# Two attention averages of one group, taken one step apart and gathered bank by bank

## The chip, the cores and the metric

The kernel runs on one core of a Trainium2 chip. Times are device microseconds of one execution, as a median of several runs; less is better. The trace comes from one further execution under the hardware profiler.

## The reference

The model is a two-layer perceiver block on 16 batches of 64 latents (width 128). Each layer has a cross-attention of the latents onto a context of 1601 rows (16 heads), then a sequence layer (a selective scan) and a feed-forward part (a mixture of experts in layer 0, quantised in layer 1). The part that the change touches is the cross-attention:

```python
xn = layernorm(context); ln = layernorm(latents)
q = ln @ Wq
k, v = split(concat([xn, ln]) @ Wkv)
w = softmax(q k^T * scale)          # per batch and head; 64 latents x 1665 keys
out = (w @ v) @ Wo
```

## The kernel before, in words

**Tiling.** Keys and queries are folded, so that scores are taken between the normalised context (transposed, `kvT`, width 128) and 8 heads x 64 latents = 512 query columns at a time. A "group" is one layer, one batch and one half of the heads: 2 x 16 x 2 = 64 groups. A group has NT = 13 key tiles of 128 rows (the last one holds 64 context rows and the 64 latents; the 1601st context row is treated apart, through `ee` and `xeb`).

**One step.** `run` (L1419) walks over steps n; step n handles tile i = n mod 13 of group g = n div 13 and calls `step` (L1562). It first issues the scores of that tile (`scores`, L643): one matmul of 512 columns into one of three PSUM banks tagged "s"; VectorE folds it into a running maximum R (L664 with a mask in layer 1, L666 without); ScalarE copies it into half of a two-tile buffer tagged "st2" (L669 or L671). There are eleven st2 buffers (and two for the single thirteenth tile). When the group is through, its maximum is transposed and reduced (`maximum`, L674, at step 1 of the next group), spread (L698, step 3), and subtracted from the stored scores, which are then exponentiated in place (`weigh`, L701: VectorE L706, ScalarE L707), a pair of tiles at a time on every second step.

**The averages.** LAG = 21 steps behind the scores, `average` (L709) multiplies the exponentials of a tile with the context rows: four matmuls of 128 queries x 129 columns (width 128 and a column of ones for the denominator), accumulated over the group's 13 tiles. Two of the four blocks lie in one PSUM bank and two in another, and both banks are one tile, `av`, of which there is one. After the thirteenth tile, `gather` (L721) adds the row treated apart and moves the four blocks to SBUF (four VectorE instructions, L728). The first tile of a group is not averaged in its own step but together with the second (`ia` 0 and 1). Seen by the step's position in the 13, the last averages of a group are in step 7, step 8 has none, and step 9 has those of tiles 0 and 1 of the next group.

**After it.** Thirteen steps behind, `denominator` (L764: reciprocal on VectorE, product on Pool), `turn` (L770: four transposes) and, after each second batch, `output` (L785: 32 matmuls, L791, and VectorE's sum into X, L795) follow at fixed steps. The last group of all has its own end, `finish` (L732).

**What sets the order.** `scores` and `average` are issued in the text's order; the compiler's planner then orders each engine's instructions by its own model, as far as data and the hand-made ordering edges (`behind`, L1545) allow. Background work is put between: preparation of contexts by due step (`prep`), and the sequence and feed-forward layers, once their inputs are done (`between`, with due steps from `done`, L1426). A batch's context lies in `kv`, of which there are three buffers; the next load (`context_load`, L468, with Pool's memset L472 and SP's DMA L486 or L489) waits until the averages of three batches before are through. In layer 0, `context` (L576) then begins with VectorE's reduce over the rows loaded (L606).

Of the kernel before, what the change touches and what calls it, by code (L numbers as in the profile page):

```python
# [32 lines left out]
F32 = mybir.dt.float32  # L33
# [4 lines left out]
ALU = mybir.AluOpType  # L38
# [4 lines left out]
P = 128  # L43
NB, L, D = 16, 64, 128
# [8 lines left out]
NT = G + 1  # L53
NQ = 512
LAG = 21
# [24 lines left out]
class Kernel:  # L80
# [236 lines left out]
    def raw_pair(self, lay, l, r, g, queue):  # L317


        if lay == 0:  # L320
            t = self.at.tile([P, 2, NQ], F32, tag="st2", name=f"raw{l}{g}", bufs=11)
            pair = [t[:, i, :2 * D].rearrange("p (m d) -> p m d", m=2) for i in range(2)]
        else:
            pair = [self.at.tile([P, 2, D], F32, tag="raw", name=f"raw{n}{g}", bufs=3) for n in (l, r)]
        for t, n in zip(pair, (l, r)):
            queue.dma_start(out=t, in_=self.a[f"L{lay}{n}"].rearrange("(m p) d -> p m d", p=P)[:, 2 * g:2 * g + 2, :])
        return pair
# [140 lines left out]
    def context_load(self, lay, b):  # L468
        nc = self.nc
        kv = self.at.tile([P, G + 1, D + 1], F32, tag="kv", name=f"kv{lay}_{b}", bufs=3)  # L470
        kvT = self.at.tile([P, SK + L], F32, tag="kvT", name=f"kvT{lay}_{b}", bufs=2)
        nc.gpsimd.memset(kv[:, :, D:], 1.0)  # L472
        if lay == 0:
            ctxd = self.a["ctx"]
            tiles = ctxd[b, :P * G, :].rearrange("(p g) d -> p g d", g=G)
            nc.gpsimd.memset(kv[64:P, G, :D], 0.0)
            if b == 0:

                self.raw_kv = [self.at.tile([P, 2, NQ], F32, tag="st2", name=f"rkv{j}", bufs=11).rearrange("p i (g d) -> p (i g) d", d=D) for j in range(2)]
                for lo in range(0, G, 4):  # L480
                    nc.sync.dma_start(out=self.raw_kv[lo // 8][:, lo % 8:lo % 8 + 4, :], in_=tiles[:, lo:lo + 4, :])
                    if lo == 0:
                        self.raw0.append(self.raw_pair(0, "WqT", "WkT", 1, nc.sync))
                nc.sync.dma_start(out=self.raw_kv[1][:REM, G - 8, :], in_=ctxd[b, P * G:SK, :])
            else:
                nc.sync.dma_start(out=kv[:, :G, :D], in_=tiles)  # L486
                nc.sync.dma_start(out=kv[:REM, G, :D], in_=ctxd[b, P * G:SK, :])
        else:
            nc.sync.dma_start(out=kv[:, :, :D], in_=self.xh[b])  # L489
            nc.sync.dma_start(out=kvT[:, :SK], in_=self.xhT[b])  # L490
        self.kv_of[lay, b] = (kv, kvT)

    def first_context(self):


        nc = self.nc
        kv, kvT = self.kv_of[0, 0]
        w1 = self.vecs_of(0)[0]
        n = G + 1
# [22 lines left out]
        def turned(lo, hi):  # L522
            m, w = (P, (hi - lo) * P) if hi < n else (REM, REM)
            t = self.tp(f"kt0_{lo}")
            for k in range(lo, hi):
                nc.tensor.transpose(t[:, (k - lo) * P:(k - lo) * P + m], kv[:m, k, :D], self.ident[:m, :m])

            for i, j in ((0, P), (P, w)) if lo == 0 else ((0, w),):
                nc.scalar.activation(kvT[:, lo * P + i:lo * P + j], t[:, i:j], AF.Copy, scale=self.vcol[:, w1:w1 + 1])
            raw = self.at.tile([P, 2, NQ], F32, tag="st2", name=f"xt{lo}", bufs=11)[:, 0, :w]  # L530
            nc.vector.tensor_copy(raw, t[:, :w])
            nc.sync.dma_start(out=self.xhT[0][:, lo * P:lo * P + w], in_=raw)

# [109 lines left out]
    def scores(self, g, i):  # L643

        nc, grp = self.nc, self.groups[g]
        lay, b, half = grp["key"]
        if i == 0:
            grp["st"] = []
            grp["R"] = self.at.tile([P, NQ], F32, tag="R", name=f"R{g}", bufs=2)
        if i % 2 == 0:  # L650
            n = min(2, NT - i)
            grp["st"].append(self.at.tile([P, n, NQ], F32, tag=f"st{n}", name=f"st{g}_{i // 2}", bufs=11 if n == 2 else 2))
        st, R = grp["st"][i // 2][:, i % 2, :], grp["R"]
        q = self.q_of[lay, b][:, half * 8:half * 8 + 8, :].rearrange("p h l -> p (h l)")
        s = self.pss.tile([P, NQ], F32, tag="s", name=f"s{g}_{i}")
        mm = nc.tensor.matmul(s, self.kv_of[lay, b][1][:, i * P:(i + 1) * P], q, start=True, stop=True)  # L656
        self.place["PE"].append(mm.ins)
        masked = lay == 1
        mc = self.mcol[:, i, b:b + 1] if masked else None

        if i:
            last = grp["st"][0][:, 0, :] if i == 1 else R
            if masked:
                mx = nc.vector.scalar_tensor_tensor(R, s, mc, last, ALU.add, ALU.max)  # L664
            else:
                mx = nc.vector.tensor_tensor(R, s, last, ALU.max)  # L666
            self.place["DVE"].append(mx.ins)
        if masked:
            ev = nc.scalar.activation(st, s, AF.Identity, bias=mc)  # L669
        else:  # L670
            ev = nc.scalar.copy(st, s)  # L671
        self.place["ACT"].append(ev.ins)
# [33 lines left out]
        nc.vector.tensor_tensor(st, st, self.row(mb, [P, n, NQ]), ALU.subtract)  # L706
        nc.scalar.activation(st, st, AF.Exp)  # L707

    def average(self, g, i):  # L709


        nc, grp = self.nc, self.groups[g]
        lay, b, half = grp["key"]
        if i == 0:
            grp["av"] = self.psa.tile([P, 2, NQ], F32, tag="av", name=f"av{g}")
        for k in range(4):
            o = grp["av"][:, k // 2, k % 2 * (D + 1):(k % 2 + 1) * (D + 1)]
            st = grp["st"][i // 2][:, i % 2, k * P:(k + 1) * P]
            nc.tensor.matmul(o, st, self.kv_of[lay, b][0][:, i, :], start=(i == 0 and k % 2 == 0), stop=(i == NT - 1 and k % 2 == 1))  # L719

    def gather(self, g):  # L721

        nc, grp = self.nc, self.groups[g]
        aq = grp["aq"] = self.at.tile([P, 4, D + 1], F32, tag="aq", name=f"aq{g}", bufs=2)
        xeb = self.xeb_of[grp["key"][:2]]
        for k in range(4):
            o = grp["av"][:, k // 2, k % 2 * (D + 1):(k % 2 + 1) * (D + 1)]
            nc.vector.scalar_tensor_tensor(aq[:, k, :], xeb, grp["ee"][:, k:k + 1], o, ALU.mult, ALU.add)  # L728
        for k in ("st", "R", "av", "mb"):
            grp.pop(k)  # L730

    def finish(self, g):  # L732


        nc, grp = self.nc, self.groups[g]
        lay, b, half = grp["key"]
        b1 = self.vecs_of(lay)[1]
        aq = self.at.tile([P, 4, D + 1], F32, tag="aq", name=f"aq{g}", bufs=2)
        xeb, av = self.xeb_of[lay, b], grp["av"]
        blocks = av[:, :, :2 * (D + 1)].rearrange("p k (j d) -> p k j d", j=2)  # L740
        four = lambda v: v.rearrange("p (k j) -> p k j", k=2)
        den, rd = self.sm([P, 4], "den"), self.sm([P, 4], "rd")
        nc.vector.tensor_tensor(four(den), blocks[:, :, :, D], four(grp["ee"]), ALU.add)
        nc.vector.reciprocal(rd, den)
        turned = []
        for k in range(4):
            nc.vector.scalar_tensor_tensor(aq[:, k, :D], xeb[:, :D], grp["ee"][:, k:k + 1], blocks[:, k // 2, k % 2, :D], ALU.mult, ALU.add)
        for k in range(4):
            nc.scalar.activation(aq[:, k, :D], aq[:, k, :D], AF.Copy, scale=rd[:, k:k + 1])
            at = self.pss.tile([P, NQ], F32, tag="s", name=f"at{g}_{k}") if k < 3 else self.tp(f"at{g}_{k}")  # L750
# [7 lines left out]
            else:  # L758
                nc.scalar.activation(to, at, AF.Identity, bias=self.vcol[:, b1:b1 + 1])
        self.output(lay, b // 2, 1)  # L760
        for k in ("st", "R", "av", "mb"):
            grp.pop(k)

    def denominator(self, g):  # L764
# [654 lines left out]
    def run(self, out):  # L1419
# [3 lines left out]
        ng = len(self.groups)  # L1423
        per_layer = NB * 2 * NT
        start = lambda lay, b: lay * per_layer + b * 2 * NT
        done = lambda lay, b: start(lay, b) + LAG + 9  # L1426
        self.place = {"PE": [], "ACT": [], "DVE": [], "SP": [], "Pool": []}
        ahead = self.setup()

# [35 lines left out]
                    if next(between[0][2], None) is None:  # L1465
                        between.pop(0)

        self.summed, self.upto_sums = False, upto_sums
        n, go, budget, finished = 0, 0, 0.0, 0
        while n < (ng + 1) * NT + LAG + 8 or between:  # L1470
            for lay in range(2):
# [90 lines left out]
    def step(self, n, ng):  # L1562
# [1 line left out]
        if g < ng:  # L1564
            self.scores(g, i)

        ga, ia = divmod(n - LAG, NT)
        if 0 <= ga < ng and ia:
            if ia == 1:
                self.average(ga, 0)  # L1570
            self.average(ga, ia)
            if ia == NT - 1:
                if ga == ng - 1:
                    self.upto_sums()
                    self.finish(ga)
                else:
                    self.gather(ga)

        for p in (g - 2, g - 1):
            o = n - (p + 1) * NT  # L1580
# [12 lines left out]
        if 0 <= d < ng:  # L1593
            lay, b, half = self.groups[d]["key"]
            if d == ng - 1:
                return
            with self.behind():
                if o == 0:
                    self.denominator(d)
                elif o == 4:  # L1600
                    self.turn(d)
                if o == 7 and b % 2 and half:
                    self.output(lay, b // 2)
                elif o == 9 and d == ng - 2:
                    self.output(lay, b // 2, 0)


# [55 lines left out]
```

## Time and profile before

| what | value |
|---|---|
| median of 3 runs | 1988.09 us (1985.63 to 1988.84) |
| the profiled execution's own time | 1984.66 us |
| its span, first to last instruction | 1983.0 us |
| mean granted TensorE clock | 0.999 |
| averages, L719, 6656 matmuls | 866.3 us busy |
| scores, L656, 1664 matmuls | 850.6 us busy |
| gathers, L728, 252 instructions | 72.0 us busy, 341 ns each |
| subtract, L706 / exponential, L707 | 505.2 us / 445.6 us busy |

How to read it: PE is TensorE's matmul row and PEld its weight loads, which lie beside matmuls; DVE is VectorE, ACT ScalarE, POOL Pool, SP the engine that issues most DMAs. A matmul on 32-bit floats shows as two instructions. In a line such as "s L656 <- ACT st L671" the engine's instruction of line 656, writing tile s, waited for ScalarE's instruction of line 671. Matmuls overlap in their pipeline, so their cost is read from the distance between starts, not from their length.

### The profile page before, as it was taken

To read this page: it belongs to the slowest core of one execution; us is meant where nothing else is said; L and a number is where in the kernel's file an instruction comes from. 1 tells how busy PE (TensorE), PEld (TensorE's weight loads), DVE (VectorE), ACT (ScalarE), POOL (GpSimd) and SP (SyncE) were. 2 spreads that over 40 slices of the span, in tenths; PEclk is the share of its full clock that TensorE was granted. 3 is DMA by queue.
4 is the path that set the end of the run, shared out by engine and by line. 5 is a ranking of instruction groups with operands and counts; after the bars stand their busy time and mean duration, and the time that the engine had idled before them with its cause. 6 is when DMAs were issued, how large, how long until landed. Compare 5 with 4: busy or idle time off the path is not lost. (4 is left out here: it accounts for less than half of the span.)

```text
span 1983.0 us, 32835 instructions
## 1 busy us (share of the span) xinstructions
PE 1938.7 (98%) x12083; PEld 1476.6 (74%) x12083; DVE 1557.6 (79%) x2976; ACT 1380.2 (70%) x2642; POOL 516.1 (26%) x579
## 2 busy tenths in 40 slices
PE   8999999999999999999999999999999999999998
PEld 5777777677777767768777777777778777787787
DVE  6977667977868787775998778898786878777885
ACT  5787778887768888656766667776665656765561
POOL 5211122543113552121542202442110121101000
PEclk9999999999999999999999999999999999999999
DMA  6121112322122121221221112221120211101000
GB/s 178 51 68 43 46 53 77 92 58 70 29 81 85 60 82 53 66 79 45 68 82 53 41 32 71 70 58 53 49 67 2 58 37 37 42 17 37 24 1 22
DMA packets 144110, 110.82 MB, mean 56 GB/s; under 512 B 13762, under 2 KB 130254, under 8 KB 143950
## 3 DMA queue, kind: packets, MB, share of 16 engines
q1 hardware_dynamic: 143406, 108.46, 18.8%
q8 instruction: 96, 1.57, 0.3%
q14 instruction: 64, 0.52, 0.1%
q10 hardware_dynamic: 544, 0.26, 0.0%
HBM read 80.23 MB, written 27.41 MB: 54 GB/s over the span
## 5 line engine op out<-in xcount | busy, mean ns | idle before, releaser
L719 PEld LDWEIGHTS av<-kv,st 128*128 128x128 f32 x6656 | 853.3, 192 | 324.0 <-issue 305.9
L719 PE MATMUL av<-kv,st 128*128 128x129 f32 x6656 | 866.3, 275 | 3.2 <-DVE aq L728 2.5
L656 PE MATMUL s<-qT,kvT 128*128 128x512 f32 x1664 | 850.6, 599 | 16.0 <-ACT st L671 8.7
L707 ACT ACTIVATE st<-st 128x1024 f32<-128x1024 f32 (+1 forms) x448 | 445.6, 999 | 113.2 <-DVE st L706 110.4
L706 DVE TENSOR_TENSOR st<-st,mb 128x1024 f32<-128x1024 f32 (+1 forms) x448 | 505.2, 1133 | 19.8 <-PE mb L698 19.8
L669 ACT ACTIVATE st<-s,mcol 128x512 f32<-128x512 f32 x416 | 283.8, 683 | 217.3 <-DVE R L664 173.5
L671 ACT COPY st<-s 128x512 f32<-128x512 f32 x416 | 240.5, 580 | 132.5 <-DVE R L666 101.1
L656 PEld LDWEIGHTS s<-qT,kvT 128*128 128x128 f32 x1664 | 258.7, 191 | 77.9 <-ACT st L671 28.3
L664 DVE SCALAR_TENSOR_TENSOR R<-s,mcol,R 128x512 f32<-128x512 f32 x352 | 261.8, 744 | 42.3 <-PE s L656 40.8
L666 DVE TENSOR_TENSOR R<-s,R 128x512 f32<-128x512 f32 x352 | 240.5, 683 | 44.4 <-PE s L656 43.7
L570 POOL TENSOR_TENSOR kv<-kv,vec 128x384 f32<-128x384 f32 (+1 forms) x128 | 132.2, 1054 | 169.3 <-DMA xh<-kv 63.9
L768 POOL TENSOR_TENSOR aq<-aq,rd 128x512 f32<-128x512 f32 x63 | 71.4, 1134 | 354.6 <-DVE rd L767 349.3
L872 POOL TENSOR_TENSOR db<-sc_u,bb 128x512 f32<-128x512 f32 x64 | 84.6, 1324 | 141.0 <-DVE h L883 86.1
L889 POOL TENSOR_TENSOR sc_y<-sc_y,h 128x512 f32<-128x512 f32 x60 | 86.0, 1434 | 98.1 <-DVE h L888 81.5
L883 DVE TENSOR_TENSOR_SCAN h<-da,db 128x512 f32<-128x512 f32 x64 | 82.3, 1286 | 0.0
L621 ACT ACTIVATE kv<-kv,coff,crstd 128x128 f32<-128x128 f32 x182 | 76.3, 492 | 4.1 <-POOL coff L618 4.1
L612 ACT ACTIVATE scr<-kv,cmean 128x128 f32<-128x128 f32 x182 | 73.0, 401 | 3.0
L666 DVE TENSOR_TENSOR R<-s,st 128x512 f32<-128x512 f32 x32 | 22.0, 687 | 66.7 <-PE s L656 54.6
L135 POOL TENSOR_TENSOR crstd<-cvar,neghalf 128x13 f32<-128x13 f32 x14 | 34.2, 2440 | 152.0 <-DVE cvar L616 152.0
L728 DVE SCALAR_TENSOR_TENSOR aq<-xeb,ee,av 128x129 f32<-128x129 f32 x252 | 72.0, 341 | 1.0 <-PE av L719 0.8
L455 PE MATMUL q<-xnT,wqk 128*128 128x128 f32 x512 | 69.5, 278 | 0.3
L455 PEld LDWEIGHTS q<-xnT,wqk 128*128 128x128 f32 x512 | 63.1, 192 | 8.5 <-issue 3.0
(409 smaller groups left out, 1927.8 us busy)
## 6 DMA issues: line engine op xcount, KB each, us to landing
bb<-bcd SPq DMA_DIRECT2D x64, 256.0 KB, 4.6
xh<-kv SPq DMA_DIRECT2D x16, 832.0 KB, 4.8
kv<-xh SPq DMA_DIRECT2D x16, 832.0 KB, 5.6
kvT<-xhT SPq DMA_DIRECT2D x16, 800.0 KB, 4.6
xhT<-kvT SPq DMA_DIRECT2D x15, 800.0 KB, 3.4
kv<-in_ctx_dram SPq DMA_DIRECT2D x15, 768.0 KB, 5.5
ew<-in_e1T_dram SPq DMA_DIRECT2D x36, 64.0 KB, 1.8
ew<-in_e3T_dram SPq DMA_DIRECT2D x36, 64.0 KB, 1.9
```

The lines of the kernel that those rows point to most:

```text
L455: nc.tensor.matmul(t[:, k * P:(k + 1) * P], self.wqk[:, g * 4 + k, :], xnT, start=True, stop=True)
L570: nc.gpsimd.tensor_tensor(kv[:, lo:hi, :D], kv[:, lo:hi, :D], self.row(self.vec[:, w1, :], [P, hi - lo, D]), ALU.mult)
L656: mm = nc.tensor.matmul(s, self.kv_of[lay, b][1][:, i * P:(i + 1) * P], q, start=True, stop=True)
L664: mx = nc.vector.scalar_tensor_tensor(R, s, mc, last, ALU.add, ALU.max)
L666: mx = nc.vector.tensor_tensor(R, s, last, ALU.max)
L669: ev = nc.scalar.activation(st, s, AF.Identity, bias=mc)
L671: ev = nc.scalar.copy(st, s)
L706: nc.vector.tensor_tensor(st, st, self.row(mb, [P, n, NQ]), ALU.subtract)
L707: nc.scalar.activation(st, st, AF.Exp)
L719: nc.tensor.matmul(o, st, self.kv_of[lay, b][0][:, i, :], start=(i == 0 and k % 2 == 0), stop=(i == NT - 1 and k % 2 == 1))
L872: nc.gpsimd.tensor_tensor(db, u, self.row(bb[:, 0, s % 2, :], both), ALU.mult)
L889: nc.gpsimd.tensor_tensor(y, y, h, ALU.add)
```

## The change

The tile `av` becomes two tiles of one bank each, `av0` and `av1`. `average` takes the bank j and issues two of the four matmuls. `step` calls it for bank 0 at LAG steps behind the scores and for bank 1 at LAG + 1. `gather` takes the bank too: each bank is gathered (two instructions) right after its own last tile, bank 1 a step after bank 0. For the last group of all, bank 1's last tile is averaged in the same step as bank 0's, and `finish` follows there. `finish` reads the two tiles and computes its denominators in two instructions. There are twelve st2 buffers. `denominator`, `turn`, `output` and the due steps of the background work (`done`) move by one step.

```diff
-            t = self.at.tile([P, 2, NQ], F32, tag="st2", name=f"raw{l}{g}", bufs=11)
+            t = self.at.tile([P, 2, NQ], F32, tag="st2", name=f"raw{l}{g}", bufs=12)
...
-    def average(self, g, i):
+    def average(self, g, i, j):
...
         if i == 0:
-            grp["av"] = self.psa.tile([P, 2, NQ], F32, tag="av", name=f"av{g}")
-        for k in range(4):
-            o = grp["av"][:, k // 2, k % 2 * (D + 1):(k % 2 + 1) * (D + 1)]
-            st = grp["st"][i // 2][:, i % 2, k * P:(k + 1) * P]
-            nc.tensor.matmul(o, st, self.kv_of[lay, b][0][:, i, :], start=(i == 0 and k % 2 == 0), stop=(i == NT - 1 and k % 2 == 1))
-
-    def gather(self, g):
+            t = self.psa.tile([P, NQ], F32, tag=f"av{j}", name=f"av{g}_{j}")
+            grp["av", j] = t[:, :2 * (D + 1)].rearrange("p (k d) -> p k d", k=2)
+        for k in range(2):
+            st = grp["st"][i // 2][:, i % 2, (2 * j + k) * P:(2 * j + k + 1) * P]
+            nc.tensor.matmul(grp["av", j][:, k, :], st, self.kv_of[lay, b][0][:, i, :], start=(i == 0 and k == 0), stop=(i == NT - 1 and k == 1))
+
+    def gather(self, g, j):
...
-        aq = grp["aq"] = self.at.tile([P, 4, D + 1], F32, tag="aq", name=f"aq{g}", bufs=2)
-        xeb = self.xeb_of[grp["key"][:2]]
-        for k in range(4):
-            o = grp["av"][:, k // 2, k % 2 * (D + 1):(k % 2 + 1) * (D + 1)]
-            nc.vector.scalar_tensor_tensor(aq[:, k, :], xeb, grp["ee"][:, k:k + 1], o, ALU.mult, ALU.add)
+        if j == 0:
+            grp["aq"] = self.at.tile([P, 4, D + 1], F32, tag="aq", name=f"aq{g}", bufs=2)
+        xeb, av = self.xeb_of[grp["key"][:2]], grp.pop(("av", j))
+        for k in range(2):
+            nc.vector.scalar_tensor_tensor(grp["aq"][:, 2 * j + k, :], xeb, grp["ee"][:, 2 * j + k:2 * j + k + 1], av[:, k, :], ALU.mult, ALU.add)
...
-        nc.vector.tensor_tensor(four(den), blocks[:, :, :, D], four(grp["ee"]), ALU.add)
+        for j in range(2):
+            nc.vector.tensor_tensor(den[:, 2 * j:2 * j + 2], av[j][:, :, D], grp["ee"][:, 2 * j:2 * j + 2], ALU.add)
...
-        done = lambda lay, b: start(lay, b) + LAG + 9
+        done = lambda lay, b: start(lay, b) + LAG + 10
...
-        ga, ia = divmod(n - LAG, NT)
-        if 0 <= ga < ng and ia:
+        for j in range(2):
+            ga, ia = divmod(n - LAG - j, NT)
+            if not 0 <= ga < ng or not ia:
+                continue
+            end = ga == ng - 1 and ia == NT - 1
+            if j and end:
+                continue
             if ia == 1:
-                self.average(ga, 0)
-            self.average(ga, ia)
-            if ia == NT - 1:
-                if ga == ng - 1:
-                    self.upto_sums()
-                    self.finish(ga)
-                else:
-                    self.gather(ga)
+                self.average(ga, 0, j)
+            self.average(ga, ia, j)
+            if end:
+                self.late_half = ga
+            elif ia == NT - 1:
+                self.gather(ga, j)
+        if self.late_half is not None:
+            self.average(self.late_half, NT - 1, 1)
+            self.upto_sums()
+            self.finish(self.late_half)
+            self.late_half = None
...
-                if o == 0:
+                if o == 1:
                     self.denominator(d)
-                elif o == 4:
+                elif o == 5:
                     self.turn(d)
-                if o == 7 and b % 2 and half:
+                if o == 8 and b % 2 and half:
                     self.output(lay, b // 2)
-                elif o == 9 and d == ng - 2:
+                elif o == 10 and d == ng - 2:
                     self.output(lay, b // 2, 0)
```

More of the change, by code (lines that the diff above doesn't have):

```diff
@@ L477, in context_load @@
             if b == 0:
-                self.raw_kv = [self.at.tile([P, 2, NQ], F32, tag="st2", name=f"rkv{j}", bufs=11).rearrange("p i (g d) -> p (i g) d", d=D) for j in range(2)]
+                self.raw_kv = [self.at.tile([P, 2, NQ], F32, tag="st2", name=f"rkv{j}", bufs=12).rearrange("p i (g d) -> p (i g) d", d=D) for j in range(2)]
                 for lo in range(0, G, 4):
@@ L529, in turned @@
                 nc.scalar.activation(kvT[:, lo * P + i:lo * P + j], t[:, i:j], AF.Copy, scale=self.vcol[:, w1:w1 + 1])
-            raw = self.at.tile([P, 2, NQ], F32, tag="st2", name=f"xt{lo}", bufs=11)[:, 0, :w]
+            raw = self.at.tile([P, 2, NQ], F32, tag="st2", name=f"xt{lo}", bufs=12)[:, 0, :w]
             nc.vector.tensor_copy(raw, t[:, :w])
@@ L651, in scores @@
             n = min(2, NT - i)
-            grp["st"].append(self.at.tile([P, n, NQ], F32, tag=f"st{n}", name=f"st{g}_{i // 2}", bufs=11 if n == 2 else 2))
+            grp["st"].append(self.at.tile([P, n, NQ], F32, tag=f"st{n}", name=f"st{g}_{i // 2}", bufs=12 if n == 2 else 2))
         st, R = grp["st"][i // 2][:, i % 2, :], grp["R"]
@@ L714, in average @@
         if i == 0:
-            grp["av"] = self.psa.tile([P, 2, NQ], F32, tag="av", name=f"av{g}")
-        for k in range(4):
-            o = grp["av"][:, k // 2, k % 2 * (D + 1):(k % 2 + 1) * (D + 1)]
-            st = grp["st"][i // 2][:, i % 2, k * P:(k + 1) * P]
-            nc.tensor.matmul(o, st, self.kv_of[lay, b][0][:, i, :], start=(i == 0 and k % 2 == 0), stop=(i == NT - 1 and k % 2 == 1))
-    def gather(self, g):
-        nc, grp = self.nc, self.groups[g]
-        aq = grp["aq"] = self.at.tile([P, 4, D + 1], F32, tag="aq", name=f"aq{g}", bufs=2)
-        xeb = self.xeb_of[grp["key"][:2]]
-        for k in range(4):
-            o = grp["av"][:, k // 2, k % 2 * (D + 1):(k % 2 + 1) * (D + 1)]
-            nc.vector.scalar_tensor_tensor(aq[:, k, :], xeb, grp["ee"][:, k:k + 1], o, ALU.mult, ALU.add)
-        for k in ("st", "R", "av", "mb"):
-            grp.pop(k)
+            t = self.psa.tile([P, NQ], F32, tag=f"av{j}", name=f"av{g}_{j}")
[4 more added lines that the diff above has]
+    def gather(self, g, j):
+        nc, grp = self.nc, self.groups[g]
+        if j == 0:
[3 more added lines that the diff above has]
+            nc.vector.scalar_tensor_tensor(grp["aq"][:, 2 * j + k, :], xeb, grp["ee"][:, 2 * j + k:2 * j + k + 1], av[:, k, :], ALU.mult, ALU.add)
+        if j:
+            for k in ("st", "R", "mb"):
+                grp.pop(k)
     def finish(self, g):
@@ L738, in finish @@
         aq = self.at.tile([P, 4, D + 1], F32, tag="aq", name=f"aq{g}", bufs=2)
-        xeb, av = self.xeb_of[lay, b], grp["av"]
-        blocks = av[:, :, :2 * (D + 1)].rearrange("p k (j d) -> p k j d", j=2)
-        four = lambda v: v.rearrange("p (k j) -> p k j", k=2)
+        xeb, av = self.xeb_of[lay, b], [grp.pop(("av", j)) for j in range(2)]
         den, rd = self.sm([P, 4], "den"), self.sm([P, 4], "rd")
-        nc.vector.tensor_tensor(four(den), blocks[:, :, :, D], four(grp["ee"]), ALU.add)
+        for j in range(2):
+            nc.vector.tensor_tensor(den[:, 2 * j:2 * j + 2], av[j][:, :, D], grp["ee"][:, 2 * j:2 * j + 2], ALU.add)
         nc.vector.reciprocal(rd, den)
@@ L746, in finish @@
         for k in range(4):
-            nc.vector.scalar_tensor_tensor(aq[:, k, :D], xeb[:, :D], grp["ee"][:, k:k + 1], blocks[:, k // 2, k % 2, :D], ALU.mult, ALU.add)
+            nc.vector.scalar_tensor_tensor(aq[:, k, :D], xeb[:, :D], grp["ee"][:, k:k + 1], av[k // 2][:, k % 2, :D], ALU.mult, ALU.add)
         for k in range(4):
@@ L760, in finish @@
         self.output(lay, b // 2, 1)
-        for k in ("st", "R", "av", "mb"):
+        for k in ("st", "R", "mb"):
             grp.pop(k)
@@ L1466, in upto_sums @@
                         between.pop(0)
-        self.summed, self.upto_sums = False, upto_sums
+        self.summed, self.upto_sums, self.late_half = False, upto_sums, None
         n, go, budget, finished = 0, 0, 0.0, 0
```

## The prediction, on record before the result was known

> **What bounds the kernel now.** I read the page first, for the shares of the engines, then TensorE's waits and those of the engines that feed it, then the timeline of one boundary between two groups, and last the distance from every matmul's start to the next one's over the whole trace.
>
> The page's first part (engine, busy us, share, instructions):
>
> ```profile
> PE 1938.7 (98%) x12083; PEld 1476.6 (74%) x12083; DVE 1557.6 (79%) x2976; ACT 1380.2 (70%) x2642; POOL 516.1 (26%) x579
> ```
>
> TensorE is busy for 1938.7 of 1983.0 us. Everything else has a fifth or more of its time free. So the end is set by TensorE's instruction stream, and a change that leaves its 12083 matmuls as they are can only win or lose at TensorE's stalls. Which stalls? TensorE's own waits, longest first (line that waited, releaser, total us, times, longest):
>
> ```profile
> PE s L656 <- ACT st L671: 8.7, 15, 1.2
> PE s L656 <- ACT st L669: 6.6, 10, 1.9
> PE av L719 <- DVE aq L728: 2.5, 6, 0.9
> ```
>
> and from the same view over all engines:
>
> ```profile
> ACT st L669 <- DVE R L664: 173.5, 163, 6.5
> ...
> ACT st L671 <- DVE R L666: 101.1, 102, 4.6
> ...
> DVE cmean L606 <- DMA kv<-in_ctx_dram: 10.4, 9, 2.1
> ```
>
> Two kinds lead: a score that waits for ScalarE to empty its PSUM bank (the three "s" banks), and a first average that waits for VectorE's gather. ScalarE's copy in turn waits for VectorE's maximum on the same bank. So the first kind is also VectorE being late. Where that happens is seen in the timeline at 1216 to 1223 us (start, duration, engine, line, operation):
>
> ```profile
> 1215.77 1.88 PE L656 MATMUL s<-qT,kvT 128*128 128x512 f32 x4
> ...
> 1217.02 0.34 DVE L728 SCALAR_TENSOR_TENSOR aq<-xeb,ee,av 128x129 f32<-128x129 f32 x1
> 1217.28 0.68 DVE L207 SCALAR_TENSOR_TENSOR sc_dt<-sc_dt,sp_ln 128x512 f32<-128x512 f32 x1
> 1217.88 0.86 DVE L728 SCALAR_TENSOR_TENSOR aq<-xeb,ee,av 128x129 f32<-128x129 f32 x3
> 1218.66 0.74 DVE L664 SCALAR_TENSOR_TENSOR R<-s,mcol,R 128x512 f32<-128x512 f32 x1
> 1218.79 1.34 ACT L669 ACTIVATE st<-s,mcol 128x512 f32<-128x512 f32 x2
> ...
> 1219.51 1.12 PE L656 MATMUL s<-qT,kvT 128*128 128x512 f32 x2 [1.86 <-ACT st L669]
> ...
> 1220.47 2.84 PE L719 MATMUL av<-kv,st 128*128 128x129 f32 x24
> ```
>
> Two scores, then a third that stands still for 1.86 us, then three averages in a row. VectorE spends the time on the four gathers, and the maximum that frees the bank comes after them. This is a boundary: steps 8 and 9 of a group in the text's order hold no average or two (tile 0 is done together with tile 1, because the bank pair is not free before the gather), and in the trace the third score is often pulled ahead too: in 31 boundaries three scores stand between the last average and the first of the next group, in 33 boundaries two.
>
> Size of it: a score is two matmuls at 0.43 us from start to start, an average eight at 0.112 (0.89). Taking from each start-to-start distance the usual one for that line and shape leaves 106 us over the span, start and tail included. In the 61 boundaries of groups 2 to 62, the score of step 9 holds 7.1 us of it, that of step 10 12.4 us, the first average 5.9 us. Over all other steps the scores stall 11 us together. So the change has about 25 us to work on.
>
> **The change, part by part.** Write a and b for the averages on the first and second bank (four matmuls, 0.45 us each) and s for a score (0.86).
>
> *Order.* Before, from step 7: s7 a12+b12, s8, s9 a0+b0 a1+b1, s10 a2+b2, with the third score often ahead. After: s7 a12 b11, s8 b12, s9 a0 a1, s10 a2 b0 b1, s11. The matmuls are the same in number and shape: 0 us. Against the three scores in a row, s9 starts 0.45 us later after s8 and s10 0.45+0.89 = 1.33 us later, filled with work that had to be done anyway. So at each boundary a stall of s9 shrinks by up to 0.45 us and the two stalls together by up to 1.33. Boundary by boundary this credits 15.6 of the 19.4 us. But VectorE must still do the same work: with 21% of its time free and a step of 2.30 us (score 22 at 53.1 us, score 831 at 1914.3) it catches up under 0.5 us per step, and some of the lateness will meet a later score. I keep three quarters: **-11.7 us**.
>
> *Gather by bank.* Four STT of 0.34 us (L728) stay four: 0 us on VectorE. But a0 now waits for two of them, not four, and between a12 and a0 stand b11, s8, b12, s9 = 2.6 us where two or three scores stood (1.7 or 2.6). The worst stall of a first average is 1.14 us; two STT less and the extra cover take it: **-5.9 us**. b0 has more cover (s9, a0, a1, s10, a2: 3.5 us).
>
> Here a rule of the Trainium skill would give another sum. "Perfetto Trace Analysis", section Optimizing Tensor Performance, Matmuls, says that independent matmul groups should rotate through different PSUM banks so that emptying one lies beside the next one's matmuls. Before, the pair is emptied with no average beside it: by the rule 63 gathers of four, 1.12 us each, are exposed, some 71 us. The trace says 5.9 us, since the scores lie beside it; I take the trace. The same page's rule (Identifying the Most-Contended Engine) that matmul busy time misleads and weight-load busy time measures headroom would give 26% of the span, 506 us; the start-to-start distances speak against it: of 5913 distances between averages' matmuls the median is 112 ns and the sum above it 3.0 us. The stream is dense.
>
> *Last boundary.* With no scores left, the chain of work that ended last runs through the gather of the last group but one:
>
> ```profile
> 1923.90 0.97 issue
> 1925.28 1.05 DVE aq L728 x4
> 1926.47 7.61 PE av L719 x66
> ```
>
> Now only two STT precede a0 and b12 lies beside them: **-1.0 us**, half of the two lines. The last group's second bank is completed in the same step as before, so the end is no step later; its denominator takes two small VectorE instructions in place of one, near the 0.17 us of a reciprocal on the same shape: **+0.15 us**.
>
> *Twelve buffers.* A pair's exponentials now stay one step longer. With eleven, pair 0's buffer was wanted by step 10's copy right after step 9's average freed it; ScalarE waited for that four times (7.7 us, two of them at the start). With twelve it is wanted three steps later, against a release one step later. 0 us, perhaps 1 us gained.
>
> *One step later.* The denominator, turn and output of a group move one step together with the gather that they follow; the output's 32 matmuls fall into step 3, behind the four transposes that spread the maximum, and VectorE's sum into X waits behind them there in place of step 2. Its price was paid before (VectorE waits 40.6 us for it in all, and TensorE doesn't stand still for it): 0 us. The background work starts a step later, far from the end: 0 us.
>
> *Context buffers.* This is the cost. The three kv buffers are freed by a batch's last average, now b12: s and half an average later, 1.30 us. In layer 0 the load for batch b (b from 3) is already issued the moment its buffer comes free (free at 269.6, issued at 269.6, landed at 274.9) on SP's queue, where scan inputs and output rows queue behind it, and behind Pool's memset, and VectorE's reduce (L606) stands still for the landing nine times. All that is queued behind that reduce on VectorE, the next maxima, waits with it, and through ScalarE's copy the scores. Lower bound 0: the waits so far, up to 2.1 us, left no stall of TensorE behind them in all but one case, and the reduce may be placed a step later. Upper bound 13 loads by 1.30 = 16.9 us. The nearest row is the wait itself; only the waits near 2 us (three of them) would pass what three banks can bridge: 3 by 1.30, of which I take half: **+2 us**.
>
> Sum: -11.7 -5.9 -1.0 +0.15 +2 = -16.4 us. The profiled execution took 1984.66 us (span 1983.0 and 1.7 around it), so 1968.2 for its like; it lies 3.4 us below the median 1988.09 of runs from 1985.63 to 1988.84. From the median: **1971.7 us**.
>
> **Rivals.** (1) *The backlog stays.* VectorE's late maxima are not caused by the clump of scores but by the other work that shares it (in the timeline above a row of the background scan, L207, lies between the gathers). Then the stall moves from s9 and s10 to s11 and s12, and only the first averages and the last boundary gain: -5.9 -1.0 +2 = -5, 1983 us. For it: 79% busy on average, and s10's stall is often several instructions deep. Against: steps 0 to 8 of every group, with the same VectorE load but spaced scores, stall only 6 us together. (2) *More than that.* The spacing also calms steps 11 and 12, where 5 us of score stalls and some of the transposes' waits lie, and buffers no longer hold ScalarE: all 25 us and up to 5 more, 1958 to 1963. (3) *Slower: the kv chain.* If VectorE keeps the reduce where it is in its order, each of the 13 loads delays it by the full 1.30 us, and in layer 1 Pool's scaling, which waits 35.5 us for 16 such loads, passes its delay on through the weighted context: 13 by 1.30 plus 16 by 1.30 = 38 us of delay. It decides from where more than half of that reaches the scores while the clump's gain is as small as in (1): +19 -7 = +12, 2000 us. Against: those waits leave no stall now. (4) *The order isn't the written one.* The trace's third score ahead of the averages shows that the order on TensorE is planned. If the plan pulls s10 ahead of a0 again, the clump is back and only the gather's half remains: about -3, 1985 us. Against: what held a0 back in the plan is now two STT with 2.6 us of other work in front.
>
> **How the numbers follow.** Main case, 1966 to 1978 us: 0.50. More (2): 0.12. Backlog stays (1): 0.16. Order unchanged (4): 0.08, on the border of no change. Slower (3): 0.14. The measurement can tell about 0.2%, 4 us, from no change. Faster by more than that: main, (2), and most of (1): 0.72. Within: the rest of (1), most of (4): 0.13. Slower: (3) and a little of (4): 0.15. The range takes in (1) and the cases of faster and cuts (3) off and the far end of (2): 1960 to 1990.
>
> **What would show it.** Right: in the changed trace no three scores in a row, "s L656 <- ACT st" waits of TensorE (15.3 us in sum) down by half or more, "av L719 <- DVE aq L728" near nothing, busy time of TensorE the same within some us. Backlog: the same waits, at steps 11 and 12. Kv chain: "cmean L606 <- DMA" well over 10.4 us with stalled scores right behind. The prediction fails if VectorE's order at the boundary changes so that the gathers still come before the maxima of two scores.

## The result and the profile after

The changed kernel takes 1975.2 us (median of 6 runs, 1974.18 to 1980.0) against 1987.58 us before (6 runs beside it); ratio 0.9944, interval 0.9933 to 0.9954. That is 11 to 12 us faster, where the prediction had 16.4. A second set of runs of the same kernel, further down, gives 0.9940.

The page's first part, after:

```profile
PE 1940.9 (98%) x12083; PEld 1485.0 (75%) x12083; DVE 1573.0 (80%) x2977; ACT 1386.7 (70%) x2642; POOL 512.5 (26%) x579
```

The same 12083 matmuls, the same busy time within 2.2 us: the work on TensorE is unchanged, as was claimed, and the time came out of its stalls. TensorE's own waits, longest first:

```profile
PE s L656 <- ACT st L671: 6.4, 7, 2.1
PE av L719 <- DVE aq L728: 4.2, 6, 1.3
...
PE s L656 <- ACT st L669: 0.4, 1, 0.4
```

Scores that wait for ScalarE went from 15.3 us to 6.8. The first average that waits for the gather went the other way, from 2.5 to 4.2. Counting every start-to-start distance against the usual one for its line and shape, over the 61 boundaries of groups 2 to 62, gives the sizes (us); the first average's count before depends on what is taken as usual, and with medians it is 5.0 and not 5.9:

| stalled instruction | before | after | after, second set |
|---|---|---|---|
| score of step 9 | 7.1 | 4.2 | 4.5 |
| score of step 10 | 12.4 | 3.2 | 3.2 |
| first average (step 9) | 5.9 | 6.7 | 6.7 |

In the trace the score of step 10 stands ahead of the first average at 2 boundaries, not 31 (group 29, with a longer row of scores in both traces, is left out), and there too the second bank's last tile lies between the scores. The profiled execution itself took 1978.93 us (span 1977.2), 3.7 more than the median. Part of that lies in stretches in which TensorE was granted half its clock; the last section shows them.

The timeline of one boundary after the change, at 413 to 418 us (TensorE and VectorE rows):

```profile
414.00 1.02 PE L656 MATMUL s<-qT,kvT 128*128 128x512 f32 x2
414.11 1.21 DVE L883 TENSOR_TENSOR_SCAN h<-da,db 128x512 f32<-128x512 f32 x1
...
414.86 0.61 PE L719 MATMUL av<-kv,st 128*128 128x129 f32 x4
415.24 1.19 DVE L706 TENSOR_TENSOR st<-st,mb 128x1024 f32<-128x1024 f32 x1
415.30 1.02 PE L656 MATMUL s<-qT,kvT 128*128 128x512 f32 x2
...
416.95 0.60 DVE L728 SCALAR_TENSOR_TENSOR aq<-xeb,ee,av 128x129 f32<-128x129 f32 x2
...
417.61 1.16 PE L719 MATMUL av<-kv,st 128*128 128x129 f32 x8 [1.28 <-DVE aq L728]
```

The order is the written one: score, four matmuls of the second bank's last tile, score, then the first bank's next two tiles. What fails is the time of the gather. The first bank was complete at 414.0 us, but VectorE came to its two instructions at 416.95, after a scan step (L883), a subtraction (L706) and a maximum, and the first average stood for 1.28 us. Group 14, whose boundary this is, has an output in its step 3; with the output a step earlier the first average does not stall here, as the experiment on the output's step shows.

### The profile page after: what moved, and what is told of

The parts are those of the page before. It is cut to its first block, busy times and chain, and to the rows that moved or that the text cites. A ratio compares the mean times of both kernels' runs of the same rounds, so it can differ in the third digit from the quotient of the medians.

```text
span 1977.2 us, 32791 instructions
## 1 busy us (share of the span) xinstructions
PE 1940.9 (98%) x12083; PEld 1485.0 (75%) x12083; DVE 1573.0 (80%) x2977; ACT 1386.7 (70%) x2642; POOL 512.5 (26%) x579
## 5 line engine op out<-in xcount | busy, mean ns | idle before, releaser
L719 PEld LDWEIGHTS av<-kv,st 128*128 128x128 f32 x6656 | 870.2, 192 | 376.9 <-issue 356.9
L719 PE MATMUL av<-kv,st 128*128 128x129 f32 x6656 | 882.8, 275 | 4.6 <-DVE aq L728 4.2
L656 PE MATMUL s<-qT,kvT 128*128 128x512 f32 x1664 | 860.2, 599 | 7.6 <-ACT st L671 6.4
L706 DVE TENSOR_TENSOR st<-st,mb 128x1024 f32<-128x1024 f32 (+1 forms) x448 | 503.7, 1134 | 17.7 <-PE mb L698 17.7
L889 POOL TENSOR_TENSOR sc_y<-sc_y,h 128x512 f32<-128x512 f32 x60 | 80.9, 1348 | 116.2 <-DVE h L888 102.6
L883 DVE TENSOR_TENSOR_SCAN h<-da,db 128x512 f32<-128x512 f32 x64 | 93.2, 1456 | 0.6 <-ACT da L871 0.6
L728 DVE SCALAR_TENSOR_TENSOR aq<-xeb,ee,av 128x129 f32<-128x129 f32 x252 | 76.2, 341 | 0.0
```

What stands on the lines that cost most here:

```text
L719: nc.tensor.matmul(grp["av", j][:, k, :], st, self.kv_of[lay, b][0][:, i, :], start=(i == 0 and k == 0), stop=(i == NT - 1 and k == 1))
L883: nc.vector.tensor_tensor_scan(flat(h), flat(da), flat(db), 0.0, ALU.mult, ALU.add)
```

## The experiments

The experiments were measured in three sets, each beside the kernel before: its median was 1984.71 us for the first four, 1986.31 for the next four and 1987.4 for the last four. All differences below are the ratio to the kernel before of the same set, times 1986 us.

**Twelve buffers alone.** Edit: in the kernel before, all four of

```diff
-tag="st2", ..., bufs=11
+tag="st2", ..., bufs=12
```

> The kernel before with twelve st2 buffers and nothing else. Theory of spacing (the gain comes from scores and averages that alternate at the boundary, with each bank gathered by itself): 0 to -1 us, ScalarE's 7.7 us of waits for an average gone and TensorE's score stalls unchanged near 34 us. Rival (the buffers are the gain: ScalarE no longer holds a score's bank while it waits for a buffer): -8 us or more.

Measured: ratio 1.0001 (0.9990 to 1.0011). ScalarE's waits for an average are gone from its list, and the time is the same. The buffers are not the gain.

**Banks apart, no step between them.** Edit to the changed kernel, with its due steps and buffers set back to those of before:

```diff
-            ga, ia = divmod(n - LAG - j, NT)
+            ga, ia = divmod(n - LAG, NT)
```

> Two tiles of one bank, each gathered by itself, but both banks averaged at the same step as before; eleven buffers. Theory of spacing: the first average needs only two gathers, so its own stall (5.9 us) goes and the planner pulls the third score ahead less often, but steps 8 and 9 still hold two scores with nothing between: -3 to -6 us of the change's -12. Rival (rotating the banks is the whole gain): -10 us or more.

Measured: 0.9986 (0.9979 to 0.9993), -2.8 us. Three scores in a row are left at 4 boundaries only and step 10's stall falls from 12.4 to 2.7 us, but step 9's stays (7.8) and the first average's too (6.0). So one bank's gather alone ends the pulling ahead, and is worth a quarter of the change. The stalls of steps 9 and 10 together fell by 9.0 us and the time by 2.8: a recount of the two traces finds the rest again as stalls elsewhere, 1.3 us at the score of step 7 and the others on many lines, none of them more. A stall that goes at one place is not yet time.

**Eleven buffers in the changed kernel.** Edit: the four `bufs=12` back to `bufs=11`.

> The changed kernel with eleven st2 buffers. Pair 0's buffer is then wanted by step 10's copy, and is freed by the second bank's averages of tiles 0 and 1, which stand behind that score in the same step. Theory of spacing: ScalarE waits for an average at many boundaries, 0.5 to 1 us each, which holds copies and with them scores: 5 to 15 us slower than the changed kernel, so between -7 and +3 against before. Rival (the twelfth buffer is decoration): equal to the changed kernel, -12.

Measured: 0.9942 (0.9927 to 0.9957), -11.5 us, the changed kernel's own time. My theory fell here and the rival held. The waits that I expected are there, in ScalarE's list:

```profile
ACT st L669 <- PE av L719: 13.0, 13, 1.6
ACT st L671 <- PE av L719: 1.7, 4, 1.3
```

14.7 us of them cost nothing that the times show. The likely cover is that after step 10's score come three half averages, and the next score needs another bank; no run shows this.

**Both banks gathered together, with the step between them.** Edit to the changed kernel:

```diff
-            elif ia == NT - 1:
-                self.gather(ga, j)
+            elif ia == NT - 1 and j:
+                self.gather(ga, 0)
+                self.gather(ga, 1)
```

> The changed kernel, but both banks are gathered together after the second bank's last tile. The spacing of the scores is that of the change; the first bank is free only a step later. Theory: the first average then stalls or the third score is pulled ahead again, and half the gain or more goes: -6 to +5 us. Rival (the spacing alone is the gain, the gather by bank adds nothing): -10 to -12 us.

Measured: 0.9975 (0.9967 to 0.9984), -5.0 us. The score of step 10 is ahead of the first average again at 12 boundaries, the first average's stall is 11.7 us, step 10's 5.9. TensorE's waits name it:

```profile
PE av L719 <- DVE aq L728: 6.8, 9, 1.8
```

Banks alone -2.8, step alone -5.0, both -11 to -12: together they are worth 3 to 4 us more than the two by themselves. The two runs are not equal in all else, though. Gathering both banks after the second one's last tile leaves the first bank less cover than it had before, and this kernel has the output in step 3, which the kernel before has in step 2 (see below).

**All averages one step later.** Edit: the kernel before with twelve buffers and `LAG = 22`.

> The kernel before with twelve buffers and LAG 22: every average one step later, nothing else. It is the price of being a step late (context buffers freed later, background later) without the gain. Twelve buffers alone were worth 0. Prediction's term: +2 us. Rival (kv chain): +10 us or more, with VectorE's waits for the context's DMA well over 10 us. Third possibility: below 0, then a step later is itself no cost.

Measured: 1.0019 (1.0010 to 1.0027), +3.8 us; its trace is not read here. By itself it reads like the price I named. But at LAG 22 the output of a pair of batches also falls into step 3, and the kernel with that move alone (below) is +3.6 us. The averages' later step, and with it the later release of the context buffers, is left with 0.2 us. The intervals of the two runs leave some 2 us either way, so the +2 of the prediction is not excluded; the +10 of its rival is.

**The changed kernel with LAG 20.** Edit: `LAG = 20`.

> The changed kernel with LAG 20: the first bank one step earlier than before, the second where it was, so the context buffers come free as before. If the later release costs the change anything, this is faster than the changed kernel by that, 2 us by the prediction's term. If the release costs nothing: equal within 2 us, -9 to -13 against before.

Measured: 0.9959 (0.9943 to 0.9975), -8.1 us. Context buffers come free as before, and it is not faster but some 3 us slower than the changed kernel. The intervals of this run and of the changed kernel's overlap a little; a second kernel with LAG 20, below, gives the same.

**The second bank two steps behind.** Edit to the changed kernel, with due steps one later again and the last group's end completed with two tiles:

```diff
-        for j in range(2):
-            ga, ia = divmod(n - LAG - j, NT)
+        for j in (1, 0) if (n - LAG) % NT == 1 else (0, 1):
+            ga, ia = divmod(n - LAG - 2 * j, NT)
```

> The changed kernel with the second bank two steps behind; in step 9 its last tile goes ahead of the first bank's next two. The first average then has 3.1 us of other matmuls between it and the last one on its bank, against 2.6. Theory (the first average's 6.7 us of stall are VectorE reaching the gather late, so cover helps): its stall falls to 3 us or less, and the time to -13 to -17 against before. Rival (the lateness follows TensorE, since the smoother stream only runs ahead of VectorE): the stall moves to another score or average and the time stays at -10 to -13.

Measured: 0.9978 (0.9970 to 0.9987), -4.4 us. The first average's stall does fall, from 6.7 to 1.3 us. The score stalls rise: step 8 from 0.9 to 3.1, step 9 from 4.5 to 7.6, step 11 from 4.3 to 8.0. The stall moves to other scores, as the rival had it, but the time went up by some 7 us over the changed kernel's, which neither had. Its cause is not isolated, since the run also frees the context buffers later and reorders step 9. VectorE's wait for the context's DMA is also up here (16.4 us against 8.6), the only trace read here in which it clearly rose.

**The changed kernel again.**

> The changed kernel once more, on the chip and beside the kernel before of the three others, as what they are compared with: -11 to -13 us. Theories don't differ on it.

Measured: 0.9940 (0.9927 to 0.9954), -11.9 us.

**The output's step.** Reading the traces side by side showed a row that I had put at zero: VectorE's wait for the 32 output matmuls, 40.6 us before, is after

```profile
DVE X L795 <- PE o L791: 2.0, 1, 2.0
```

since the sum into X now stands behind subtractions that VectorE does meanwhile. Is this a hidden gain? Four corners were measured: with and without the step between the banks, output in step 2 or 3. The edit in the kernel before, and its reverse in the changed one, is

```diff
-                if o == 7 and b % 2 and half:
+                if o == 8 and b % 2 and half:
```

> The kernel before, with only the output of a pair of batches (32 matmuls and VectorE's sum into X) moved from step 2 to step 3, as the change moves it. In the changed kernel VectorE's wait for these matmuls fell from 40.6 us to 2.0, since subtractions now stand ahead of the sum. Theory of spacing and banks: VectorE's free time in step 2 or 3 is not what TensorE waits for: 0 to -1 us. Rival (the output's move is a hidden part of the gain): -3 to -6 us.

> The changed kernel with the output left in step 2. VectorE's wait for the output should be back near 40 us. Theory of spacing and banks: -11 to -12 against before, as the changed kernel. Rival (output): -6 to -8.

> Banks gathered each by itself, no step between them (-2.6 with the output in step 2), with the output in step 3: the fourth corner of step shift by output. Theory of spacing and banks: -2.6 to -4. Rival (output): -6 to -9. If shift and output add up, shift is worth the changed kernel less this one.

| | output in step 2 | output in step 3 |
|---|---|---|
| kernel before | 0 | +3.6 (1.0018, 1.0012 to 1.0025) |
| banks apart, no step | -2.8 | +1.8 (1.0009, 1.0000 to 1.0017) |
| banks apart and a step | -11.3 (0.9943, 0.9931 to 0.9956) | -11.1 and -11.9 |

The wait itself behaves as expected: with the output back in step 2 of the changed kernel it reads

```profile
DVE X L795 <- PE o L791: 35.2, 14, 3.7
```

and the time is the same. So 33 us of VectorE standing still are worth nothing there: not a hidden gain. What the trace does show is a price that the times are too coarse for. With the output back in step 2, TensorE's wait for the gather reads

```profile
PE av L719 <- DVE aq L728: 2.2, 3, 1.0
```

against 4.2 us in six waits with it in step 3, and the first average's stall, counted as above, is 4.1 us and not 6.7. Nearly all of the difference lies at the boundaries with an output. At the boundary shown above VectorE then comes to the gather 0.79 us after the score of step 8 starts, not 2.95, and the first average doesn't stall. The interval of that run (-13.7 to -8.7 us) does not tell 2.6 us from nothing. Without the step the move even costs 3.6 and 4.6 us, which neither theory had. The step between the banks is worth 8.5 us with the output in step 2 and about 13 in step 3. The step without the banks, -5.0 with the output in step 3, is 8.6 less than the kernel before with the output there too.

**LAG 20 with the output in step 3.** Edits: `LAG = 20`, `o == 9` for the output, and the layer 1 fold of the output weights two steps later.

> The changed kernel with LAG 20, which came out at -8, and its output moved from step 2 to step 3. If the output's step is what it lacked: -12, or -14 if the earlier release of the context buffers adds something. If LAG 20 is short of the change for another reason (its boundary lies in other steps): -8 still.

Measured: 0.9960 (0.9946 to 0.9973), -7.9 us: LAG 20 is short of the change for another reason than the output.

## Why the prediction was right, and where its terms were off

- **Bound and order of size: right.** TensorE's stream is dense, its busy time didn't move, and the gain is stalls that went. The time lies in the range, on the side forecast.
- **Order, -11.7: right.** Step 9's and 10's stalls went from 19.4 to 7.4 us, -12.0. That it needs both parts is shown by the two kernels that have one of them: each takes 9 us or more from the same stalls, and they win 2.8 and 5.0 us of time. The three quarters that I kept were a guess, so that the size is so near is partly luck.
- **Gather by bank, -5.9: wrong.** This is the step that failed: "two STT less and the extra cover take it". The first average's stall is 6.7 us, not 0; 4.1 of it are there with the output in step 2 too, so the term by itself won about 1 us (5.0 to 4.1, with medians), and the output's move put 2.6 on top. The gather did become shorter (1.23 us from its first start to its last end on average, now 0.62 for a bank) and the next first average did come later (3.27 us from the start of the last average on its bank, now 3.65). But VectorE came to the gather later: 1.11 us after the start of the last average before, at worst 2.85; now 1.44 and 3.5. Group 12 shows the exchange: its boundary had 0.99 us of stall at the scores of steps 9 and 10 and none at the first average; now it has none at these scores, but 0.82 at the average and 1.17 at the score of step 11. Where TensorE used to wait for VectorE at the score, it runs on and meets the same lateness an instruction or two later. The kernel with two steps between the banks confirms it from the other side: more cover before the first average moves the stall back to the scores. I had kept a quarter of the scores' credit for this backlog and none of the average's, where part of it came due.
- **Last boundary, -1.0: it came, and was lost again just behind.** Before, TensorE stood 0.49 us before four background matmuls (L903) and 0.40 us before the last group's first average; after, it stands at neither. But right behind these averages it now waits 0.62 us for another VectorE instruction (L1339), which it didn't before. From the last score's start to the end are 68.2 us before and 68.7 after, 0.45 of it because four more matmuls of the averages lie behind that score; within that, the denominator's +0.15 can't be told apart.
- **Context buffers, +2: no cost seen.** Averages a step later cost 0.2 us, give or take 2, once the output's step is taken out, VectorE waits 9.3 us for the context's DMA against 10.4, and releasing the buffers earlier (LAG 20) won nothing. That the planner moves the reduce along with its data would explain it; no run isolates that.
- **Twelve buffers, 0: right**, though not for the reason given. I thought them needed for the step; with eleven the changed kernel is as fast.
- **The output's move, 0: right in this kernel's time** by the run that undoes it, to within 2.5 us; in the trace it costs the first averages 2.6 us, and it costs 3.6 us of time in the kernel before. "Its price was paid before" was no reason: VectorE no longer waits for the output's matmuls, yet at the boundaries with an output it comes later to the gather that TensorE waits for.

With the wrong terms set to what was measured (first average +0.8, or +1.7 with medians, context buffers 0, last boundary 0) the sum is -11.7 + 0.8 + 0.15 = -10.8, or -9.9, against -11.1 and -11.9. That is a fit after the fact and not a test. The slower rival did not come, and the backlog rival came in part, at the first average instead of at steps 11 and 12: step 11's stall, counted with medians of neighbouring pairs, is 4.6 us before and 4.2 after.

What stays open: why LAG 20 is some 3 us behind LAG 21, and why the output in step 3 costs 3.6 us without the step. For LAG 20 no place stands out, and one of its two traces is as short as the changed kernel's second (span 1973.5 against 1973.2). For the output, one wait stands out: in both kernels without the step TensorE waits 1.3 and 1.4 us for the DMA of layer 1's output weights (L344), a wait that the same kernels with the output in step 2 don't have; the rest is spread. A fourth context buffer, which would test the release directly, was not measured.

## What to carry to other kernels

When the bounding engine's stalls come from another engine's backlog, credit a removed stall only with what the other engine can catch up until the next instruction that needs it, whichever that is. Here the boundary's three stalls fell from 25.4 us to 14.1, and the first average, which was to be freed, kept its own or took on more. Spacing the bounding engine's demands and splitting the release (bank by bank) were worth 5.0 and 2.8 us alone and 11 to 12 together, so such pairs are tested as corners, not one by one. And a long wait in the list of an engine that isn't the bound (here 33 us of VectorE) can be worth nothing at all.

## What the hardware showed that was not expected

In this profile TensorE's granted clock falls to half for a stretch of about 3.4 us after a hole in its work, though no single stall is as long as that. Busy time of the engines in stretches of 4 us, changed kernel (the columns: total, busy time of PE, PEld, DVE, ACT, POOL, granted clock, DMA share, GB/s):

```profile
710.00:714.00 4.00, 3.76 (x18) 2.47 (x18) 4.00 (x6) 3.99 (x11) 0.90 (x1) 1.00 0.01 2
714.00:718.00 4.00, 1.78 (x10) 0.97 (x8) 4.00 (x10) 0.58 (x2) 3.74 (x4) 1.00 0.00 0
718.00:722.00 4.00, 3.17 (x9) 2.14 (x10) 2.61 (x5) 4.00 (x11) 2.12 (x2) 0.57 0.00 0
```

At 714 to 718 us TensorE is busy for 1.78 us, and in the next stretch it runs at 0.57. The rows of the timeline show who held it:

```profile
714.49 2.44 POOL L135 TENSOR_TENSOR crstd<-cvar,neghalf 128x13 f32<-128x13 f32 x1
...
717.81 0.49 ACT L621 ACTIVATE kv<-kv,coff,crstd 128x128 f32<-128x128 f32 x1 [3.42 <-POOL coff L618]
...
718.83 2.07 PE L656 MATMUL s<-qT,kvT 128*128 128x512 f32 x2 [2.10 <-ACT st L671]
```

ScalarE stood 3.42 us for Pool's power (2.44 us) and the product behind it (L618, 0.77 us), with the score's copy next in its order, and the score's two matmuls, normally 1.02 us from first start to last end, then took 2.07. In the kernel before the same place has stretches of 2.87 and 2.79 us of 4 busy, and the clock there stays at 1.00:

```profile
715.00:719.00 4.00, 2.87 (x13) 1.56 (x13) 4.00 (x7) 4.00 (x11) 1.95 (x2) 1.00 0.00 0
723.00:727.00 4.00, 2.79 (x19) 2.12 (x19) 2.62 (x4) 4.00 (x11) 2.06 (x2) 1.00 0.53 122
```

The busy share alone does not decide, though: from 1679.0 to 1682.4 us that kernel's TensorE is busy for 1.05 us of 3.4, and its clock stays at 1.00. The changed kernel's profile holds three such half-clock stretches after its start (3.4 us at 39 and 718 us, 6.8 us at 1609), about 6.8 us lost by an estimate that counts half of each; the profile of before holds none until its last 3 us. The second trace of the changed kernel holds 10.2 us of half clock where this one holds 13.7, and its execution took 1974.9 us, so about 1.7 us of the 4.0 between them are of this kind. The mean clock and the time go together from run to run: of the kernel before, in the second set, 14 runs with a mean clock of 0.997 average 1989.1 us and 16 with 0.999 average 1984.4. By the stretch at 718 us, a stall of 2.1 us at an unlucky place costs nearly twice itself (an estimate: half of the 3.4 us on top), and sets of runs with different mean clocks are compared with care when the difference is a few microseconds.

The Trainium skill ("TensorE: Matmul & The Clock Gate", What's actually happening) describes such a gate, with a window of 3.4 us and half the clock after an idle window. The length of the stretches agrees; here TensorE was still busy 45% of the 4 us before.
